# Bias rows of the first image's attention loaded and turned in separate steps, the opening reordered, and one later use in layer 1

## The chip, the cores and the metric

The kernel runs on one core of one Trainium2 chip. The metric is the device time of one execution in microseconds (us); lower is better. It ran three times: 3124.01 us in the median, 3123.47 at the lowest and 3126.42 at the highest. One further execution was recorded by the hardware profiler, and every duration of a single instruction comes from that one.

The core has engines that run side by side, each working through its own instructions in the order of the program: TensorE (PE, with its weight loads as PEld), VectorE (DVE), ScalarE (ACT), GpSimd (POOL) and SyncE (SP), which here issues nearly all the DMAs. They meet only at semaphores.

## What is computed

The input is 8 images of 384 channels with 32 x 32 pixels, that is 1024 tokens of 384 numbers each. Two layers follow one another. Everything is float32.

```
# layer 0, per image
x = x + attn0(group_norm(x))          # 8 heads of 48
#   attn = softmax(q k^T / sqrt(48) + bias[head, query, key]) ; out = attn v ; out @ proj_w + proj_b
#   bias = MLP(relative position of query and key)   -- the same for all images

# layer 1, on tokens t
t = t + attn1(layer_norm(t))          # 6 heads of 64
#   q = (q - mean) / std, k = (k - mean) / std over the 64 numbers of a head (ddof 1)
#   attn = softmax(q k^T / sqrt(64)) ; out = attn v ; out @ proj_w.T + proj_b
t = t + ffn(layer_norm(t))            # sign weights, absmax-quantised activations, GELU
#   the quantisation covers images 0 to 4; for images 5 to 7 the ffn gives zero
```

The bias depends only on the difference of two positions. So there are just 63 x 63 = 3969 values for each head: a small MLP over a table of positions makes them, and every score finds its bias by its offset in the table.

## The kernel before

**Units.** The attention of one image is cut into units `(pair, h, m2)`: a pair of heads, a half of the queries, and a quarter of the keys (256). Layer 0 has 4 x 2 x 4 = 32 units an image, layer 1 has 24. `scores` of a unit makes two PSUM tiles of 128 x 1024 on PE (L513); VectorE adds the bias to each (L524) and ScalarE takes the exponential (L528). `weigh` of a unit runs two units later (`LAG = 2`) and multiplies the exponentials by the values into an accumulator (L544). When a half of the queries is complete, ScalarE and VectorE bring the accumulator into `oT` (L552, L555); when a pair is complete, `divide` sends its sums through memory, GpSimd inverts them (L573), and the result is loaded again, spread over the partitions, and multiplied into `oT`. All PSUM tiles, those of projections and accumulators too, share one pool of four buffers (`mm2`).

**Order.** The order of every engine's work is the order of the statements. A hand-written clock spreads the small work between the large: `later.after(n, work)` does `work` at the n-th following call of `later.step()`. In image 0 of layer 0, `project_qk` calls it six times (after each projection of a pair's queries or keys), `project_v` four times, and then every unit once; so unit i ends with step 11 + i. At equal steps, work is done in the order in which it was registered.

**The opening.** The first image is loaded and its group norm measured (`stages[0]` to `stages[2]`). `hidden` makes the MLP's hidden layer (L350, L355), `stages[3]` sends the norm's scale and shift through memory, `table_part` makes each half of the bias table (L366, L371) and stores it in memory (L375), and `stages[4]` applies the norm on VectorE (L440). Then the weights for values and output are loaded, and projections follow (L459 queries and keys, L487 values).

**The bias.** `grow` holds the bias in the form in which the scores read it: for each of 8 heads, 60 rows of 32. It is filled in 32 parts `(head, c)` of 15 rows. For each part, `grow_part` issues four DMAs (L387), each of which fetches 32 shifted copies of a stretch of the table into a tile `wide` (117 KB each), and then one copy reads `wide` backwards into `grow`, on ScalarE for even `c` (L393) and on VectorE for odd `c` (L395). `wide` comes from a pool of nine tiles (`etile`), which also gives the hidden layer's tiles and the exponentials. A pair of heads needs 8 parts: pair 0 from unit 0 on, pair 1 from unit 8, pair 2 from unit 16, pair 3 from unit 24.

```python
for i in range(22):
    later.after(i + 1, lambda i=i: grow_parts(2 if i < 10 else 1))
```

**The next image.** After unit 1 of each image the next one is loaded (L252), and the stages of its group norm follow 5, 6, 7, 10 and 13 steps on (three times L410, then L424 and on, then L440 on GpSimd).

**Layer 1.** `attention_inputs` (L1562, the changed call is L1584) prepares an image's queries, keys and values for images 0, 6 and 7; for the others the feed-forward of the image before does it. `head(pair, a, b)` sums the squares of a pair's queries and keys on PE (L1157), sends them through memory, and takes the inverse root on GpSimd (L1178, 5.42 us). Then `apply` loads the queries' part as `rq` (L1192) `a` steps later, and the queries are multiplied by it on VectorE (L1199) `b` steps after that. Pair 2 is the last; its queries are used from unit 16 on. Tiles named by `wtile` come from a pool of 16.

Of the kernel before, what the change touches and what calls it, by code (L numbers as in the profile page):

```python
# [19 lines left out]
F32 = mybir.dt.float32  # L20
F32R = mybir.dt.float32r
AF = mybir.ActivationFunctionType
# [5 lines left out]
P = 128  # L28
QP = P // 2
B, C, IH, IW = 8, 384, 32, 32  # L30
# [10 lines left out]
NF0 = NP0 - 1  # L41
# [3 lines left out]
RW = 2 * IW - 1  # L45
# [7 lines left out]
NP1 = H1 // 2  # L53
# [43 lines left out]
class _Shared:  # L97
# [13 lines left out]
    def mm2(self, name):  # L111
        return self.ps.tile([P, NH, HALF], F32, tag="p", name=name)
# [71 lines left out]
def _layer0(tc, ins, x1, sums, shared, beside):  # L184
# [4 lines left out]
    nc = tc.nc  # L189
# [4 lines left out]
    with ExitStack() as ctx:  # L194
        const = ctx.enter_context(tc.tile_pool(name="a_const", bufs=1))
# [7 lines left out]
        def etile(name, shape=(P, N)):  # L203
            return ep.tile(list(shape), F32, tag="e", name=name)
# [4 lines left out]
        later = _Later()  # L209
# [8 lines left out]
        def backwards(last, *dims):  # L218

            dims = [(1, n) if isinstance(n, int) else n for n in dims]  # L220
            return bass.AP(last.tensor, last.offset, [last.ap[0]] + [[-s, n] for s, n in dims])
# [13 lines left out]
        for g in range(P // QT):  # L235
            at = g * QN
            n = min(QN, NREL - at)
# [80 lines left out]
        def load_weights_v_out():  # L318
            nc.sync.dma_start(wv, qkv_w[:, 2 * C : 3 * C].rearrange("(k p) c -> p k c", p=P))
            nc.sync.dma_start(bv, qkv_b[2 * C : 3 * C].partition_broadcast(P))  # L320
            pw = ins["L0_conv_proj_w"]
            for j in range(2):
                last = (2 * NF0 + j) * D0
                for row, n, at, step in (
                    (j * S0 + SP, D0, j * D0, 2 * D0),
                    (j * S0, FR, last, FR),
                ):
                    nc.sync.dma_start(
                        wp[row : row + n],
                        bass.AP(  # L330
                            pw.tensor, pw.offset + at * C, [[C, n], [step * C, NF0], [1, C]]
                        ),
                    )
                nc.sync.dma_start(wl[j * S0 + SP : (j + 1) * S0], pw[last : last + D0])
            with nc.allow_non_contiguous_dma(reason="a bias, once"):
                nc.sync.dma_start(bp, ins["L0_conv_proj_b"].rearrange("(k p) -> p k", p=P))

        oT = kept.tile([P, NP0, N], F32, tag="oT", name="oT")

        WR = GW // 4  # L340

        def hidden(r):

            hids = {}
            for k in range(2):
                for a in range(2):
                    ph = mm2(f"ph{r}{k}{a}")
                    for i in range(2):
                        g = 2 * a + i
                        nc.tensor.matmul(  # L350
                            ph[0:HC, i], w1[g * QT : g * QT + 2, ts(k, HC)],
                            rel[g * QT : g * QT + 2, ts(r, HALF)], start=True, stop=True,
                        )
                    hid = etile(f"hid{r}{k}{a}", (HC, 2, HALF))
                    nc.scalar.activation(  # L355
                        hid.rearrange("p i q -> p (i q)"), ph[0:HC].rearrange("p i q -> p (i q)"),
                        AF.Gelu, bias=b1[:, k : k + 1],
                    )
                    hids[k, a] = hid
            return hids  # L360

        def table_part(r, hids):
            pb = mm2(f"pb{r}")
            for k in range(2):
                for g in range(P // QT):
                    nc.tensor.matmul(  # L366
                        pb[ts(g, QT), 0], w2[:, k, :], hids[k, g // 2][:, g % 2],
                        start=(k == 0), stop=(k == 1),
                    )
            part = etile(f"part{r}", (P, HALF))  # L370
            nc.vector.tensor_scalar_add(backwards(part[:, HALF - 1 : HALF], HALF), pb[:, 0], b2)  # L371
            for g in range(P // QT):
                at = g * QN + r * HALF
                n = min(HALF, NREL - at)
                nc.sync.dma_start(  # L375
                    table[:, NREL - at - n : NREL - at],
                    part[g * QT : g * QT + H0, HALF - n : HALF],
                )

        def grow_part(h, c):  # L380

            run = (WR - 1) * RW + IW
            wide = etile(f"wide{h}_{c}", (P, WR, RW))
            for dy in range(QROWS):
                src = table[h : h + 1, :]
                at = src.offset + NREL - 1 - (WR * (c + 1) + QROWS - 2 - dy) * RW - 2 * (IW - 1)
                nc.sync.dma_start(  # L387
                    wide[ts(dy, IW)].rearrange("p w c -> p (w c)")[:, :run],
                    bass.AP(src.tensor, at, [[1, IW], [1, run]]),
                )  # L390
            turned = backwards(wide[:, WR - 1, IW - 1 : IW], (RW, WR), IW)
            if c % 2 == 0:
                nc.scalar.copy(grow[:, h, ts(c, WR), :], turned)  # L393
            else:
                nc.vector.tensor_copy(grow[:, h, ts(c, WR), :], turned)  # L395
# [240 lines left out]
        hids = [hidden(r) for r in range(2)]  # L636
        stages[3]()
        load_bias_qk()
        for r in range(2):
            table_part(r, hids[r])  # L640
        stages[4](nc.vector)
        load_weights_v_out()
        parts = [(h, c) for h in range(H0) for c in range(4)]

        def grow_parts(n):
            for _ in range(n):
                grow_part(*parts.pop(0))

        for i in range(22):
            later.after(i + 1, lambda i=i: grow_parts(2 if i < 10 else 1))  # L650
        qk = project_qk(0, first)
        project_v(0, first)
        with_last = beside(etile)
        for b in range(B):
            held = []
            for i, u in enumerate(units):
                done = held.pop(0) if len(held) == LAG else None
                held.append(
                    (u, scores(b, qk, u, lambda: weigh(b, *done) if done else None))
                )  # L660
                if i == 1 and b + 1 < B:
                    xn = load(b + 1)
                    for at, stage in zip((5, 6, 7, 10, 13), group_norm(b + 1, xn)):
                        later.after(at, stage)
                if i == 3 and b > 0:
                    project_out(b - 1, residuals(b - 1, etile), range(NF0))
                if b == B - 1:
                    for at, work in with_last:
                        if at == i:
                            work()  # L670
                later.step()
            if b + 1 < B:
                qk = project_qk(b + 1, xn)
            for done in held:
                finish = weigh(b, *done)
                if finish is not None:
                    finish()
            if b + 1 < B:
                project_v(b + 1, xn)
# [8 lines left out]
    def finish():  # L688
        project_out(B - 1, rest, range(NF0, NP0))
        keep.close()  # L690
# [319 lines left out]
def _layer1(tc, ins, x1, out, shared, start, before=None, check=None):  # L1010
# [3 lines left out]
    nc = tc.nc  # L1014
    with ExitStack() as ctx:
# [4 lines left out]
        const = pool("b_const", 1)  # L1020
# [5 lines left out]
        later = _Later()  # L1026
# [37 lines left out]
        wide = room = w1 = w2 = None  # L1064
# [10 lines left out]
        tiny = const.tile([P, 2], F32, tag="tiny", name="tiny")  # L1075
# [486 lines left out]
        def attention_inputs(b, xt, rest=()):  # L1562

            d, qk, sq = head_rows(b), {}, {}
            kc = kc_tile(b)
            tk = token_sums(f"a{b}", xt, [square(f"a{b}", xt, k) for k in range(KC)])

            def head(pair, *steps):
                head_sums(b, pair, sq, d)
                normalise_qk(b, pair, qk, d, kc, steps)  # L1570

            for pair in range(NP1):
                for s in range(2):
                    project_qk(b, pair, s, xt, qk, sq)
                    if (pair, s) == (0, 1):
                        token_stats(f"a{b}", tk)
                    if s == 0 and pair > 0:
                        head(pair - 1, *((3, 3) if pair == 1 else (5, 4)))
            for work in rest:
                work()  # L1580
                later.step()
            for m2 in range(MT // 2):
                project_v(b, xt, m2, tk)
            head(NP1 - 1, 3, 2)  # L1584
            return qk, kc

        def kc_tile(b):
# [19 lines left out]
        for b in range(B):  # L1607
# [4 lines left out]
            oT = None  # L1612
# [4 lines left out]
            for i, u in enumerate(units):  # L1617
# [7 lines left out]
                if i == 3:  # L1625
# [3 lines left out]
                    oT = wide.tile([P, KC, N], F32, tag="o", name=f"oT{b}")  # L1629
# [146 lines left out]
```

## Time and profile before

| what | value |
|---|---|
| median of the runs | 3124.01 us |
| the profiled execution | 3124.0 us |
| its span, first to last instruction | 3122.2 us |
| mean granted TensorE clock | 0.993 of full |
| VectorE add of the bias, L524 | 1218 ns |
| ScalarE exponential, L528 | 1057 ns |
| turning copy, ScalarE L393 / VectorE L395 | 593 / 653 ns (medians) |
| GpSimd inverse of the sums, L573 | 2899 ns |
| PE at work in 0 to 40 us | 30.03 us |
| PE at work in 80 to 100 us | 14.89 us |
| PE at work in 120 to 140 us | 7.34 us |

A busy time of an engine is the sum over its instructions. Since matmuls are pipelined, a busy PE need not be a fast PE: the row PEclk of the page, and the clock in the windows, say what share of the full clock TensorE had. An entry such as `DVE grow L395 <- DMA wide<-table: 54.1, 13, 10.8` in the list of waits reads: VectorE stood idle before its instruction of line 395, which writes `grow`, for 54.1 us in total, 13 times, 10.8 us at the longest, and each time a DMA from `table` into `wide` came last. In the timelines the columns are the start, the time taken, the engine, the line, the operation, what it writes and reads, how many were merged into the line, and the idle time before it with what ended it.

### The profile page before, as it was taken

The numbers are of one execution on the slowest core, as the hardware profiler recorded it, in microseconds if no ns is written. First come the engines' busy times: TensorE is split into PE (matmuls) and PEld (weight loads), VectorE is DVE, ScalarE is ACT, GpSimd is POOL, SyncE is SP. The second block draws the span as 40 slices with busy tenths as digits, with TensorE's granted clock in tenths as the row PEclk, the third lists the DMA queues.
The fourth block names the chain that finished last, engine by engine and source line by source line (L and its number), as shares of the span: only waits on it lengthen the run. The fifth ranks groups of instructions, "written<-read, shape, count | busy, mean of one in ns | idle before, by whom it ended". The sixth has DMA issues, their size and how long they took to land.

```text
span 3122.2 us, 45962 instructions
## 1 busy us (share of the span) xinstructions
PE 3049.8 (98%) x19066; PEld 1579.0 (51%) x19066; DVE 1736.5 (56%) x1735; ACT 1400.7 (45%) x1762; POOL 472.9 (15%) x314
## 2 busy tenths in 40 slices
PE   8799999999999999999899999999999999999998
PEld 3254645455554645434445645545645545544343
DVE  2564727364654737364554754754754854854545
ACT  2452616253443616243463553553643543653534
POOL 0110201111110202022201201201201201211110
PEclk9899999999999999999999999999999999999999
DMA  7402020111202020222300200101101101102011
GB/s 176 113 19 80 23 77 23 48 57 20 81 20 79 23 83 16 50 72 81 92 22 16 62 22 16 62 22 26 52 22 29 49 22 29 49 16 70 16 50 43
DMA packets 102771, 150.51 MB, mean 48 GB/s; under 512 B 62260, under 2 KB 65828, under 8 KB 101784
## 3 DMA queue, kind: packets, MB, share of 16 engines
q1 hardware_dynamic: 99688, 147.41, 16.8%
q8 instruction: 153, 2.51, 0.3%
q14 instruction: 66, 0.54, 0.1%
q10 hardware_dynamic: 2864, 0.05, 0.1%
HBM read 111.05 MB, written 27.32 MB: 44 GB/s over the span
## 4 chain that ended last, share of the span: by engine, by line
PE 84%; DVE 4%; DMA 3%; ACT 2%; POOL 1%; issue 1%; SPq 1%; DVEq 0%; ACTq 0%; POOLq 0%
PE s L513 14%; PE o L544 14%; PE s L1272 10%; PE o L1321 10%; PE pq L459 7%; PE y2p L1523 5%; PE pp L608 4%; PE y1p L1469 4%; PE pq L1128 4%; PE pp L1383 4%; PE pv L487 4%; PE pv L1209 3%; POOL hc L1178 1%; PE sum L1344 1%; DMA rb<-rd 1%
## 5 line engine op out<-in xcount | busy, mean ns | idle before, releaser
L528 ACT ACTIVATE e<-e 128x1024 f32<-128x1024 f32 x512 | 535.0, 1057 | 460.0 <-DVE e L524 444.2
L524 DVE TENSOR_TENSOR e<-s,grow 128x1024 f32<-128x1024 f32 x512 | 601.0, 1218 | 192.0 <-PE s L513 190.0
L513 PE MATMUL s<-qk 48*64 48x512 f32 x4096 | 615.4, 594 | 20.9 <-DVE e L524 17.2
L544 PE MATMUL o<-e,v 64*64 64x512 f32 x4096 | 609.8, 592 | 0.0
L1283 ACT ACTIVATE e<-s,kc 128x512 f32<-128x512 f32 x768 | 463.9, 691 | 203.4 <-PE s L1272 189.5
L1321 PE MATMUL o<-e,v 64*64 64x512 f32 x3072 | 393.5, 593 | 8.8 <-DVE oT L1331 8.8
L1272 PE MATMUL s<-qk,qk 64*64 64x512 f32 x3072 | 394.2, 592 | 2.2 <-DVE v L1219 1.9
L513 PEld LDWEIGHTS s<-qk 48*64 48x64 f32 x4096 | 235.1, 133 | 254.4 <-DVE e L524 86.3
L544 PEld LDWEIGHTS o<-e,v 64*64 64x64 f32 x4096 | 255.1, 133 | 185.9 <-issue 82.4
L1298 DVE TENSOR_TENSOR t<-t,e 128x1024 f32<-128x1024 f32 x192 | 231.0, 1222 | 77.4 <-ACT e L1283 77.4
L1128 PE MATMUL pq<-bx,wqkv 128*128 128x512 f32 x576 | 254.1, 596 | 0.7 <-ACT tra L1102 0.7
L459 PE MATMUL pq<-xn,w 128*128 128x512 f32 x576 | 251.0, 597 | 1.8 <-DVE xn L440 1.8
L573 POOL TENSOR_TENSOR inv<-sums,over 128x16 f32<-128x16 f32 x32 | 92.8, 2899 | 1029.5 <-DMA sums<-sd 872.1
L1272 PEld LDWEIGHTS s<-qk,qk 64*64 64x64 f32 x3072 | 144.1, 132 | 199.4 <-issue 123.2
L1321 PEld LDWEIGHTS o<-e,v 64*64 64x64 f32 x3072 | 140.1, 133 | 199.8 <-issue 161.0
L459 PEld LDWEIGHTS pq<-xn,w 128*128 128x128 f32 x576 | 109.4, 191 | 143.4 <-issue 143.4
L1128 PEld LDWEIGHTS pq<-bx,wqkv 128*128 128x128 f32 x576 | 107.8, 190 | 143.5 <-issue 141.4
L1295 DVE TENSOR_TENSOR t<-e,e 128x1024 f32<-128x1024 f32 x96 | 114.1, 1224 | 74.5 <-ACT e L1283 74.4
L1456 DVE TENSOR_REDUCE parts<-y 128x1 f32<-128x1024 f32 x75 | 90.1, 1217 | 99.1 <-ACT y L1453 98.6
L1144 ACT ACTIVATE qsq<-pq 128x1024 f32<-128x1024 f32 x48 | 49.2, 1024 | 195.1 <-DVE qk L1138 97.2
L1178 POOL TENSOR_TENSOR hc<-hc,rsqrt 128x32 f32<-128x32 f32 x24 | 135.6, 5649 | 2.0
L1209 PE MATMUL pv<-wqkv,bx 128*128 128x384 f32 x384 | 131.1, 497 | 0.0
(147 smaller groups left out, 2937.9 us busy)
## 6 DMA issues: line engine op xcount, KB each, us to landing
rb<-rd SPq DMA_DIRECT2D x112, 256.0 KB
wide<-table SPq DMA_DIRECT2D x128, 114.2 KB
xn<-in_x_dram SPq DMA_DIRECT2D x24, 512.0 KB
res<-in_x_dram SPq DMA_DIRECT2D x24, 512.0 KB
x<-res SPq DMA_DIRECT2D x24, 512.0 KB
bx<-x SPq DMA_DIRECT2D x8, 1536.0 KB
rq<-hi SPq DMA_DIRECT2D x48, 256.0 KB
out_dram<-bx SPq DMA_DIRECT2D x24, 512.0 KB
```

Source lines behind the costliest of these rows:

```text
L459: nc.tensor.matmul(pq[:, h], wqk[:, k, s, 2 * pair : 2 * pair + 2, :].rearrange("p h d -> p (h d)"), xn[:, k, ts(h, HALF)], start=(k == 0) ...
L513: nc.tensor.matmul(s[j][ts(c, QP), i], qk[pair][rows, 1, ts(4 * m2 + 2 * i + c, QP)], qk[pair][rows, 0, ts(h, HALF)], start=True, stop=True,)
L524: nc.vector.tensor_add(e.rearrange("p (i q) -> p i q", i=2), s[j], bass.AP(near.tensor, near.offset, [near.ap[0], [-QROWS * IW, 2], [1, HA ...
L528: nc.scalar.activation(e, e, AF.Exp)
L544: nc.tensor.matmul(po[ts(j, S0), r], v[keys, 2 * m2 + i, 2 * pair + j, :], es[j][keys, ts(i, HALF)], start=(m2 == 0 and i == 0), stop=(m2 ...
L1128: nc.tensor.matmul(pq[:, h], wqkv[:, k, s * C + pair * P : s * C + (pair + 1) * P], xt[:, k, ts(h, HALF)], start=(k == 0), stop=(k == KC - 1),
L1178: nc.gpsimd.tensor_tensor(c, c, rsqrt.to_broadcast(list(c.shape)), ALU.pow)
L1209: nc.tensor.matmul(pv[:, i, 0:C], xt[:, k].rearrange("c (p m) -> c m p", m=MT)[:, 2 * m2 + i], wqkv[:, k, 2 * C : 3 * C], start=(k == 0), ...
L1272: nc.tensor.matmul(s[j][ts(c, QP), i], qk[pair, 1][rows, ts(4 * m2 + 2 * i + c, QP)], qk[pair, 0][rows, ts(h, HALF)], start=True, stop=True,)
L1283: nc.scalar.activation(e[:, ts(i, HALF)], s[j][:, i], AF.Exp, scale=kc[:, pair, j, m : m + 1])
L1298: nc.vector.tensor_add(total[j], total[j], e)
L1321: nc.tensor.matmul(po[ts(j, D1), r], v[keys, 2 * m2 + i, at : at + D1], es[j][keys, ts(i, HALF)], start=(m2 == 0 and i == 0), stop=(m2 == ...
```

## The change

There are three edits.

1. **The opening.** The norm is applied (`stages[4]`) and the weights are loaded before the bias table's first half; the second half is made one step later, after the first projection. A tile `tiny` and one exponential of it on ScalarE are added.
2. **The bias.** `grow_part` is split: `grow_load` issues the four DMAs, `grow_turn` makes the copy. Twenty parts are loaded at steps 2 to 9 (three each at the first four steps, then two) and turned one step later (first four groups) or two steps later (the rest). The other twelve are loaded one a step at steps 8 to 19 and turned one a step at steps 11 to 22; these don't use the pool of nine but three slices of `oT`, in turn. With this, image 1 is loaded after unit 8 of image 0, not after unit 1.
3. **Layer 1.** For the last pair in `attention_inputs`, the steps of `head` are (4, 4) and not (3, 2).

```diff
+        tiny = const.tile([P, 2], F32, tag="tiny", name="tiny")
+        nc.gpsimd.memset(tiny, 0.0)
...
-        def grow_part(h, c):
+        def grow_load(h, c, staged):
 
             run = (WR - 1) * RW + IW
-            wide = etile(f"wide{h}_{c}", (P, WR, RW))
+            wide = oT[:, staged, 0 : WR * RW] if staged else etile(f"wide{h}_{c}", (P, WR * RW))
             for dy in range(QROWS):
...
+            return wide
+
+        def grow_turn(h, c, wide):
+
+            last = (WR - 1) * RW + IW - 1
+            turned = backwards(wide[:, last : last + 1], (RW, WR), IW)
             if c % 2 == 0:
                 nc.scalar.copy(grow[:, h, ts(c, WR), :], turned)
...
         load_bias_qk()
-        for r in range(2):
-            table_part(r, hids[r])
         stages[4](nc.vector)
         load_weights_v_out()
+        table_part(0, hids[0])
+        later.after(1, lambda: table_part(1, hids[1]))
+        nc.scalar.activation(tiny[:, 1:2], tiny[:, 0:1], AF.Exp)
         parts = [(h, c) for h in range(H0) for c in range(4)]
-
-        def grow_parts(n):
+        waiting = []
+
+        def grow_loads(n, staged=None):
             for _ in range(n):
-                grow_part(*parts.pop(0))
-
-        for i in range(22):
-            later.after(i + 1, lambda i=i: grow_parts(2 if i < 10 else 1))
+                part = parts.pop(0)
+                waiting.append((*part, grow_load(*part, staged)))
+
+        def grow_turns(n):
+            for _ in range(n):
+                grow_turn(*waiting.pop(0))
+
+        for i, n in enumerate((3, 3, 3, 3, 2, 2, 2, 2)):
+            later.after(i + 3 + (i > 3), lambda n=n: grow_turns(n))
+            later.after(i + 2, lambda n=n: grow_loads(n))
+        for i in range(len(parts) - 20):
+            later.after(i + 11, lambda: grow_turns(1))
+            later.after(i + 8, lambda i=i: grow_loads(1, 1 + i % NF0))
...
-                if i == 1 and b + 1 < B:
+                if i == (8 if b == 0 else 1) and b + 1 < B:
                     xn = load(b + 1)
...
-            head(NP1 - 1, 3, 2)
+            head(NP1 - 1, 4, 4)
```

More of the change, by code (lines that the diff above doesn't have):

```diff
@@ L387, in grow_part @@
                 nc.sync.dma_start(
-                    wide[ts(dy, IW)].rearrange("p w c -> p (w c)")[:, :run],
-                    bass.AP(src.tensor, at, [[1, IW], [1, run]]),
-                )
-            turned = backwards(wide[:, WR - 1, IW - 1 : IW], (RW, WR), IW)
+                    wide[ts(dy, IW), 0:run], bass.AP(src.tensor, at, [[1, IW], [1, run]])
+                )
+            return wide
+        def grow_turn(h, c, wide):
+            last = (WR - 1) * RW + IW - 1
+            turned = backwards(wide[:, last : last + 1], (RW, WR), IW)
             if c % 2 == 0:
```

## The prediction

> **What bounds the kernel now.** I read the page first, then the waits and the windows of the opening 160 us, the timelines of PE, VectorE, ScalarE and SyncE there, and last the one place in layer 1 that the third edit touches. The page:
>
> ```profile
> PE 3049.8 (98%) x19066; PEld 1579.0 (51%) x19066; DVE 1736.5 (56%) x1735; ACT 1400.7 (45%) x1762; POOL 472.9 (15%) x314
> ...
> PE   8799999999999999999899999999999999999998
> ...
> PEclk9899999999999999999999999999999999999999
> ```
>
> TensorE is the bound: a microsecond counts only where PE stands still or runs at half clock. The PE row shows that in slices 1 and 2 (78 us each) and slice 20, so only the first image of layer 0 and the start of layer 1 have anything to give. Who waits for whom in 0 to 160 us (us in total, times, longest):
>
> ```profile
> ACT grow L393 <- DMA wide<-table: 55.7, 11, 18.5
> DVE grow L395 <- DMA wide<-table: 54.1, 13, 10.8
> ...
> PEld s L513 <- DVE e L524: 27.3, 14, 12.4
> ...
> PE s L513 <- DVE e L524: 17.2, 6, 11.5
> ```
>
> Each part of the bias is loaded and turned in one step, so the turning copy waits on its engine for the whole transfer, with evictions, bias adds and exponentials behind it. VectorE where units 0 and 9 of the scores stand behind a copy:
>
> ```profile
> 79.90 0.65 DVE L395 COPY grow<-wide 128x480 f32<-128x480 f32 x1 [2.42 <-DMA wide<-table]
> 80.47 1.01 DVE L492 TENSOR_TENSOR v<-pv,bv 128x384 f32<-128x384 f32 x2
> 84.06 0.65 DVE L395 COPY grow<-wide 128x480 f32<-128x480 f32 x1 [2.58 <-DMA wide<-table]
> 84.63 4.61 DVE L524 TENSOR_TENSOR e<-s,grow 128x1024 f32<-128x1024 f32 x4
> ...
> 136.80 0.65 DVE L395 COPY grow<-wide 128x480 f32<-128x480 f32 x1 [10.80 <-DMA wide<-table]
> ```
>
> The copy at 136.80 came late because SyncE stood for seven microseconds (126.03 to 132.6) inside `divide`, with the part's loads behind it. The windows (us, busy time and count of PE, PEld, DVE, ACT, POOL, granted clock, DMA share, GB/s):
>
> ```profile
> 40.00:60.00 20.00, 20.00 (x48) 8.87 (x47) 4.99 (x6) 4.40 (x6) 0.00 (x0) 1.00 1.00 220
> ```
> ```profile
> 84.00:88.00 4.00, 2.10 (x9) 0.87 (x13) 3.94 (x4) 2.05 (x3) 0.00 (x0) 0.50 0.98 324
> ...
> 134.00:138.60 4.60, 0.00 (x0) 0.00 (x0) 1.80 (x3) 0.00 (x0) 0.00 (x0) 0.50 0.63 187
> ...
> 150.00:215.40 65.40, 65.40 (x607) 37.91 (x607) 48.48 (x44) 42.29 (x44) 12.96 (x5) 1.00 0.07 18
> ```
>
> The DMA engines are full while the bias comes in, and from 150 us PE runs without a gap: 3.44 us a unit (1.72 scores, 1.72 weighing). The values' projection ends at 76.4, so without stalls units 0 to 31 would end at 76.4 + 2 x 1.72 + 30 x 3.44 = 183.0; they end at 215.4, where PE begins image 1's `pq`. So 32.4 us are lost there, and some in front. In layer 1, PE and then VectorE:
>
> ```profile
> 1539.70 2.84 PE L1272 MATMUL s<-qk,qk 64*64 64x512 f32 x16
> 1551.34 3.49 PE L1321 MATMUL o<-e,v 64*64 64x512 f32 x16 [8.79 <-DVE oT L1331]
> ```
> ```profile
> 1546.99 1.23 DVE L1199 TENSOR_TENSOR qk<-qk,rq 128x1024 f32<-128x1024 f32 x1 [7.79 <-DMA rq<-hi]
> 1548.32 2.36 DVE L1295 TENSOR_TENSOR t<-e,e 128x1024 f32<-128x1024 f32 x2
> 1550.60 0.68 DVE L1331 TENSOR_TENSOR oT<-o,oT 128x512 f32<-128x512 f32 x1
> ```
>
> The multiply by the last pair's deviations waits 7.79 us for its load; behind it stands the eviction of the weighing's accumulator, for which PE waits.
>
> **What the Trainium skill says.** "TensorE: Matmul & The Clock Gate", Architectural detail (engine queue depths): ScalarE and VectorE are strict FIFOs. The trace agrees: the ready adds of 84.63 start only after the copy. The same page, Part 1, says that after an idle window of about 3.4 us the array runs at half clock until it has been busy about as long. It agrees: PEclk is 0.50 at 84 to 92 and 134 to 142, and an L513 matmul takes 1.06 us there, 0.59 elsewhere. "DMA: Bandwidth & Descriptors", Anatomy of one DMA, says that a DMA's semaphore wait is served on the issuing sequencer; SyncE's standstill in `divide` is that.
>
> **The opening.** Applying the norm moves ahead of the table, and the table's second half behind the first projection. `pb` starts at 20.01 as before; its 32 matmuls took 6.25 us, so the first half ends at about 23.1. The scale `gsc` was issued at 17.16; image 1's was usable 1.66 us after its 0.39 us issue, so VectorE applies 19.2 to 21.6 (3 x 0.804), hidden under PE's work. `pq` starts at 23.1, not 28.05, and PE's 1.79 us gap is gone, as is the half clock of 28.7 to 32.1 (`pq`'s 72 records took 32.4 us here, 31.1 in image 1). The second half adds its 3.1 us after the first `pq`. Values' projection done: 23.1 + 31.0 + 3.1 + 15.7 = 72.9, that is 3.5 earlier. The `Exp` of `tiny` moves a 1.28 us table load from 82.62 to about 22; ScalarE waits at both, so nothing.
>
> **When parts land.** SyncE now issues the 11 weight DMAs (4.4 us) before the table stores, then waits for the second half: PE 31.4, VectorE's 0.75, four stores to 34.1, and I estimate 1.9 us to land, from the 1.66 above and the 2.45 that a late part took. First part: 36.0 + four issues 1.7 + 2.3 = 40.0 (before: 40.56). Then the engines' rate rules: before, part 19 was turned at 84.06, so (84.06 - 40.56 - 3 x 1.2 for the `qk` copies) / 19 = 2.1 us a part. Part 17 lands at about 78.6, 19 at 82.7, 20 at 84.8, 21 at 86.9, 23 at 91. Image 1's 1.5 MB, issued at 82.5 before amid the parts, now come at unit 8.
>
> **Units 0 to 4.** Turns come one to three steps behind loads, but the transfers lag the steps, so some copies still wait. (Unit i is step 11 + i.) VectorE: part 17 to 79.3, add of unit 0 to 81.7, part 19 to 83.4, unit 1 to 85.7, part 21 to 87.6, unit 2 to 89.9. ScalarE: part 20 at 84.8 precedes unit 1's exponentials. PE has four PSUM buffers, so scores of unit 3 wait for the first add of unit 2 (88.7). By then PE has been mostly idle since 74.6: half clock, and 88.7 + 3.4 for the scores + 3.4 for the weighing + 1.7 puts the end of unit 4's scores at 97.2; fully warm it would be 93.9. From there 27 units of 3.44 and one weighing: 97.2 + 92.9 + 1.7 = 191.8, or 188.5 warm. I take 191.4: 24.0 us off 215.4, the 3.5 included.
>
> **What does not come back.** Staged parts (12 of 32) use `oT` slices 1 to 3; each load waits for the copy three parts earlier, issued in the same step, which costs SyncE a short stand and leaves 10.3 us for about 4.4 us of issue and landing. The last load is issued at unit 8, the first `divide` at unit 9, so the standstill of 126 has no part behind it. The last part queues behind image 1's load: 7 us of transfer at 220 GB/s against three units; if that cover failed, VectorE would wait 1 to 3 us once. Slice 1 is first written with results at unit 13, after its last turn at unit 9. The norm of image 1 now measures at units 12 to 14 (VectorE 2.4 + 1.3 us a unit, as in later images, with buffers between) and applies at unit 20 on GpSimd, 11 units before use. Its stores and loads on SyncE meet `divide` of pair 1 at unit 17; nobody waits for either.
>
> **Layer 1.** With (4, 4) the load of `rq` is issued at unit 3 and the multiply at unit 7 instead of 2 and 4. SyncE reached that load at 1540.66, held by the chain before it and not by the step, so it lands at 1547 again; unit 7's adds come no earlier, so the wait is gone. Next late is the order that stays: exponentials of unit 5 done 1540.5, add to 1541.7, eviction 1542.4, weighing from 1542.5 instead of 1551.34: 8.8 us, plus 1.6 for the half clock that made it 3.3 us apart instead of 1.72: 10.4. Bounds: 8.8 (clock stays down) to 11.5 (PE without any gap from 1541.4). The multiply's 1.22 us in unit 7 stand before unit 8, which has no VectorE adds. Images 6 and 7 turn from unit 4 to unit 7 too, where no PE wait stood: 0.
>
> **Sum.** The profiled execution took 3124.0 us (span 3122.2, 1.8 around it), the median is 3124.01. 3124.0 - 24.0 - 10.4 = 3089.6.
>
> **Rivals.**
> 1. Transfers rule harder: the parts land 6 us later than I put them, because the table is complete later (34 instead of 28.5) and its landing is only estimated. Every unit shifts one for one: 3095.6. Against: SyncE did not start loading before 34.07 anyway.
> 2. The layer 1 edit gives nothing, because the accumulator waits for something else: 3100. Against: the three VectorE lines above follow each other without a gap.
> 3. Everything is hidden: units at PE's pace from 72.9, end at 179.5, 11.5 in layer 1: 3124.0 - 35.9 - 11.5 = 3076.6. Against: it needs part 21 at unit 1 (78 us), impossible at 2.1 us a part.
> 4. Slower: the `oT` slices are ordered as one tile, so that each staged DMA waits for the last one's landing. Place: SyncE, steps 8 to 19. Price: 4 x 2.45 = 9.8 us a part, 12 parts from 73 to 191, then 20 units: end 260, 44 us later, less layer 1's 10.4: 3158. It decides from (215.4 + 10.4 - 68.8 - 73) / 12 = 7.0 us a part. Against: the four loads of one `wide` tile go out 0.5 us apart, and `xn`'s first slice is measured while the others land.
>
> **Numbers.** Forecast 0.63 (own range 3084 to 3095: landing by 2 us either way, clock, 8.8 to 11.5), rival 1 0.17, rival 2 0.09, rival 3 0.06, rival 4 0.04, and 0.01 that gain and loss cancel. Range 3082 to 3100. A change of 0.2% (6 us) is about what this measurement can tell. Faster 0.95, same 0.01, slower 0.04.
>
> **What would show it.** Right: `pq` starting near 23; part 0 turned at 40 to 42; no VectorE wait on `wide` after 95; image 1's `pq` starting near 191; no wait before L1199 near unit 7 in layer 1. Wrong: PE gaps after unit 5, SyncE waiting long before staged loads, part 0 landing after 44, or the weighing in layer 1 still waiting for L1331.

## The result, and the profile after

The changed kernel took 3088.35 us in the median of four runs (3085.19 to 3088.45), the kernel before, beside it, 3124.82 us. The ratio is 0.9881, with a 95% interval of 0.9864 to 0.9898: 36.5 us less. The profiled execution of the changed kernel is its fastest, 3085.19 us, with a span of 3083.4; before it was 3124.0 and 3122.2. Line numbers shift: L513 is now L521, L524 is L532, L393 and L395 are L401 and L403, L387 is L391, and in layer 1 L1199 is L1220 and L1331 is L1352.

The page of the changed kernel:

```profile
PE 3039.7 (99%) x19066; PEld 1582.6 (51%) x19066; DVE 1736.9 (56%) x1735; ACT 1400.0 (45%) x1763; POOL 472.1 (15%) x315
...
PE   8999999999999999999999999999999999999998
...
PEclk9999999999999999999999999999999999999999
```

The dips of slices 2 and 20 are gone; only the very start and the very end are left. VectorE and ScalarE are busy for as long as before. The waits of its first 160 us (us in total, times, longest):

```profile
ACT grow L401 <- DMA wide<-table: 24.5, 9, 4.5
...
DVE grow L403 <- DMA wide<-table: 19.1, 8, 4.6
...
PEld s L521 <- DVE e L532: 14.4, 24, 2.8
...
PE s L521 <- DVE e L532: 2.6, 3, 1.9
```

The turning copies still wait for their parts, 45 us in all where it was 110 (1.2 us of it for parts in `oT`), but none for longer than 4.6 us, and PE waited 2.6 us for an add where it waited 17.2. VectorE at units 0 to 3, and PE where it waits for these adds:

```profile
77.33 0.65 DVE L403 COPY grow<-wide 128x480 f32<-128x480 f32 x1 [2.64 <-DMA wide<-table]
77.91 2.35 DVE L532 TENSOR_TENSOR e<-s,grow 128x1024 f32<-128x1024 f32 x2
...
84.88 0.65 DVE L403 COPY grow<-oT 128x480 f32<-128x480 f32 x1 [1.19 <-DMA oT<-table]
85.45 2.35 DVE L532 TENSOR_TENSOR e<-s,grow 128x1024 f32<-128x1024 f32 x2
88.70 2.36 DVE L532 TENSOR_TENSOR e<-s,grow 128x1024 f32<-128x1024 f32 x2 [0.91 <-PE s L521]
```
```profile
79.17 4.44 PE L521 MATMUL s<-qk 48*64 48x512 f32 x16 [1.95 <-DVE e L532]
...
86.72 1.51 PE L521 MATMUL s<-qk 48*64 48x512 f32 x11 [0.54 <-DVE e L532]
```

The copy of 84.88 is the last one on VectorE that waits for its part. The add of unit 2 stands behind it, and PE's scores of unit 3 wait for that add until 86.72. After that the adds wait for PE; the other way round there is one wait of 0.15 us, at 128.49. SyncE around the first `divide`:

```profile
107.18 1.32 SPq L252 DMA_DIRECT2D xn<-in_x_dram  x3
109.91 1.90 SPq L391 DMA_DIRECT2D oT<-table  x4
112.40 0.52 SPq L578 DMA_DIRECT2D sd<-oT  x2
115.71 0.35 SPq L580 DMA_DIRECT2D sums<-sd  x1
120.28 0.34 SPq L582 DMA_DIRECT2D rd<-inv  x1
```

It still stands for eight microseconds between 112.4 and 120.3, but the last loads of the bias went out at 109.91, ahead of it, and PE waits for nothing that is behind it. In layer 1, PE and then VectorE:

```profile
1511.84 2.92 PE L1293 MATMUL s<-qk,qk 64*64 64x512 f32 x16
1514.68 1.95 PE L1342 MATMUL o<-e,v 64*64 64x512 f32 x16
```
```profile
1513.94 0.68 DVE L1352 TENSOR_TENSOR oT<-o,oT 128x512 f32<-128x512 f32 x1
...
1523.49 1.22 DVE L1220 TENSOR_TENSOR qk<-qk,rq 128x1024 f32<-128x1024 f32 x1
```

The weighing follows the scores without a gap, the accumulator is evicted at 1513.94, and the multiply comes ten microseconds later and waits for nothing.

So the two places divide the gain like this. Image 1's first projection on PE starts at 187.16 instead of 215.40: 28.2 us. The scores before the layer 1 wait start at 1511.84 instead of 1539.70, 27.9 us, and those after it at 1516.45 instead of 1554.65, 38.2 us: 10.3 us between the two. The end keeps it: the last projection starts at 3068.76 instead of 3107.69, 38.9 us.

### The profile page after: what moved, and what is told of

It is laid out like the page before. It is cut to its first block, busy times and chain, and to the rows that moved or that the text cites. A ratio compares the mean times of both kernels' runs of the same rounds, so it can differ in the third digit from the quotient of the medians.

```text
span 3083.4 us, 45983 instructions
## 1 busy us (share of the span) xinstructions
PE 3039.7 (99%) x19066; PEld 1582.6 (51%) x19066; DVE 1736.9 (56%) x1735; ACT 1400.0 (45%) x1763; POOL 472.1 (15%) x315
## 4 chain that ended last, share of the span: by engine, by line
PE 87%; DVE 4%; DMA 3%; ACT 2%; issue 1%; SPq 1%; POOL 1%; DVEq 0%; ACTq 0%; POOLq 0%
PE s L521 14%; PE o L552 14%; PE s L1293 11%; PE o L1342 10%; PE pq L467 8%; PE y2p L1544 5%; PE pp L616 4%; PE y1p L1490 4%; PE pp L1404 4%; PE pv L495 4%; PE pq L1149 4%; PE pv L1230 3%; SPq L391 1%; PE sum L1365 1%; POOL hc L1199 1%
## 5 line engine op out<-in xcount | busy, mean ns | idle before, releaser
L532 DVE TENSOR_TENSOR e<-s,grow 128x1024 f32<-128x1024 f32 x512 | 601.4, 1218 | 190.4 <-PE s L521 189.8
L521 PE MATMUL s<-qk 48*64 48x512 f32 x4096 | 612.4, 592 | 2.7 <-DVE e L532 2.6
L521 PEld LDWEIGHTS s<-qk 48*64 48x64 f32 x4096 | 237.0, 132 | 228.5 <-issue 76.3
L1199 POOL TENSOR_TENSOR hc<-hc,rsqrt 128x32 f32<-128x32 f32 x24 | 135.4, 5642 | 2.0
```

What stands on the lines that cost most here:

```text
L521: nc.tensor.matmul(s[j][ts(c, QP), i], qk[pair][rows, 1, ts(4 * m2 + 2 * i + c, QP)], qk[pair][rows, 0, ts(h, HALF)], start=True, stop=True,)
L532: nc.vector.tensor_add(e.rearrange("p (i q) -> p i q", i=2), s[j], bass.AP(near.tensor, near.offset, [near.ap[0], [-QROWS * IW, 2], [1, HA ...
L1199: nc.gpsimd.tensor_tensor(c, c, rsqrt.to_broadcast(list(c.shape)), ALU.pow)
```

## The experiments

Each kernel ran beside the kernel before on the same chip, in three groups; medians of the kernel before were 3130.22, 3127.15 and 3124.52 us. The changed kernel ran again in the second group. "Start" is where PE begins image 1's projection in the profiled execution, which tells the first image's share apart from the rest.

| run | what it is | median us | ratio to before (95%) | start us |
|---|---|---|---|---|
| (before) | the kernel before | 3124.82 | | 215.40 |
| (after) | the changed kernel | 3088.35 | 0.9881 (0.9864 to 0.9898) | 187.16 |
| e1 | changed, layer 1 steps (3, 2) | 3099.64 | 0.9902 (0.9887 to 0.9917) | 188.18 |
| e2 | changed, image 1 loaded after unit 1 | 3089.18 | 0.9874 (0.9859 to 0.9889) | 189.08 |
| e3 | changed, old opening | 3089.50 | 0.9873 (0.9858 to 0.9888) | 188.94 |
| e4 | changed, first 20 turned at once, rest later | 3101.14 | 0.9910 (0.9896 to 0.9923) | 199.51 |
| e7 | changed, again | 3089.62 | 0.9879 (0.9864 to 0.9894) | 190.25 |
| e5 | changed, last 12 turned at once | 3101.54 | 0.9922 (0.9909 to 0.9936) | 202.46 |
| e6 | paced by landings | 3079.89 | 0.9851 (0.9837 to 0.9864) | 182.60 |
| e8 | changed, first 20 turned at once, rest by threes | 3095.61 | 0.9899 (0.9883 to 0.9914) | 195.73 |
| e9 | before, image 1 loaded after unit 8 | 3116.75 | 0.9975 (0.9964 to 0.9985) | 209.08 |
| e10 | before, layer 1 steps (4, 4) | 3114.95 | 0.9970 (0.9959 to 0.9981) | 213.48 |
| e11 | paced, GELU table early | 3077.79 | 0.9850 (0.9837 to 0.9864) | 182.22 |

### The changed kernel again (e7)

No edit.

> The changed kernel itself, as the yardstick for the others on this chip: within 0.1% of the ratio that it had, 0.988 of the kernel before.

The ratio is 0.9879. But its profiled execution starts image 1 at 190.25, 3.1 us later than the first profile. VectorE and PE in this run:

```profile
84.84 0.66 DVE L403 COPY grow<-wide 128x480 f32<-128x480 f32 x1 [1.94 <-DMA wide<-table]
...
88.04 0.65 DVE L403 COPY grow<-oT 128x480 f32<-128x480 f32 x1 [0.28 <-DMA oT<-table]
88.61 2.35 DVE L532 TENSOR_TENSOR e<-s,grow 128x1024 f32<-128x1024 f32 x2
```
```profile
89.90 1.92 PE L521 MATMUL s<-qk 48*64 48x512 f32 x16
```

The parts came later. The first one is turned at 39.82 instead of 38.87, because the first twelve `pq` took 1.1 us longer (7.61 instead of 6.55) and the table waited with them. Part 19 is turned at 84.84 instead of 80.77 and part 21 at 88.04 instead of 84.88. So the add of unit 2 is later, and the scores of unit 3, which wait for it, start at 89.90 instead of 86.72. These 3.2 us are the whole difference. Why the transfers were slower in this execution is not known.

The clock differs too. The windows of units 0 to 4 (columns as in the prediction), first of the first profile, then of this one:

```profile
73.60:90.00 16.40, 13.85 (x99) 4.44 (x102) 11.07 (x13) 8.33 (x11) 0.00 (x0) 0.90 0.89 224
```
```profile
73.60:90.00 16.40, 13.64 (x72) 3.81 (x74) 9.37 (x12) 6.43 (x9) 0.00 (x0) 0.79 0.97 237
```

PE is equally busy in both, but with a clock of 0.79 it gets through 72 matmuls instead of 99. The half clock came for 6.8 us here and for 3.4 us there. It is not what makes the difference: in both runs it lay in front of the scores of unit 3, in time that PE would otherwise have spent waiting for the add of unit 2 (its first half ended at 89.8 here). So one kernel can end three microseconds apart by when its parts land; this is about the distance between the first run of the changed kernel (3085.19) and its other three (3088.34 to 3088.45), of which no profile was taken.

### Layer 1 alone, taken back and put in (e1, e10)

```diff
-            head(NP1 - 1, 4, 4)
+            head(NP1 - 1, 3, 2)
```

> The changed kernel with the last pair's steps in layer 1 put back to (3, 2). Theory (the multiply's wait holds the accumulator's eviction, 10.3 us): slower than the changed kernel by 9 to 11.5 us, about 3098.5, with the multiply in unit 4 waiting some 7.8 us for its load again and PE idle about 8.8 us before the weighing. Rival (the wait was a by-product of when layer 0 ended, and after the earlier end the load lands in time): within 2 us of the changed kernel.

> The kernel before with the layer 1 edit alone. Theory (it is independent of the rest): faster than the kernel before by 9 to 11.5 us, as putting it back in the changed kernel cost some 10. Rival (part of it comes only together with the rest): faster by less than 7 us.

Taken back it costs 10.0 us (3099.64 to e7's 3089.62; they ran in different groups, and by the ratios it is 7.2; e2 and e3 below, which ran in its own group and equal the changed kernel, are 10.5 and 10.1 us faster than it). Put into the kernel before it gives 9.6 us (3124.52 to 3114.95). Both agree with the 10.3 of the traces. In e1 the old wait is back; PE, then VectorE:

```profile
1524.30 3.69 PE L1342 MATMUL o<-e,v 64*64 64x512 f32 x16 [8.55 <-DVE oT L1352]
```
```profile
1519.95 1.23 DVE L1220 TENSOR_TENSOR qk<-qk,rq 128x1024 f32<-128x1024 f32 x1 [7.54 <-DMA rq<-hi]
1521.28 2.36 DVE L1316 TENSOR_TENSOR t<-e,e 128x1024 f32<-128x1024 f32 x2
1523.56 0.68 DVE L1352 TENSOR_TENSOR oT<-o,oT 128x512 f32<-128x512 f32 x1
```

The multiply waits 7.54 us for `rq`, the add and the eviction follow, and PE starts the weighing when the eviction is over. The rivals (a by-product, or a gain that needs the other edits) fall.

### The last twelve parts turned in the step of their load (e5)

```diff
         for i in range(len(parts) - 20):
-            later.after(i + 11, lambda: grow_turns(1))
-            later.after(i + 8, lambda i=i: grow_loads(1, 1 + i % NF0))
+            later.after(i + 11, lambda i=i: (grow_loads(1, 1 + i % NF0), grow_turns(1)))
```

> The changed kernel with the last twelve parts loaded and turned in the same step, at steps 11 to 22 as before, still into the slices of oT; the first twenty as in the changed kernel. Theory (the loads of units 9 to 11 stand on SyncE behind divide of unit 9, which serves its waits in order): one copy at unit 9 or 10 waits 9 to 13 us, PE stands and falls to half clock, 10 to 16 us slower than the changed kernel. Rival (three slices let SyncE run ahead of the steps, so the place of the load in the order costs nothing): within 3 us of the changed kernel.

11.9 us slower than e7. SyncE, VectorE and PE:

```profile
114.89 0.52 SPq L578 DMA_DIRECT2D sd<-oT  x2
116.43 0.34 SPq L580 DMA_DIRECT2D sums<-sd  x1
121.09 0.34 SPq L582 DMA_DIRECT2D rd<-inv  x1
121.53 5.92 SPq L391 DMA_DIRECT2D oT<-table  x12
```
```profile
125.86 0.65 DVE L403 COPY grow<-oT 128x480 f32<-128x480 f32 x1 [11.01 <-DMA oT<-table]
```
```profile
127.70 2.83 PE L521 MATMUL s<-qk 48*64 48x512 f32 x11 [10.63 <-DVE e L532]
```

The three parts of units 9 to 11 (12 DMAs) leave SyncE only after `rd`, which waits for GpSimd. The copy waits 11.01 us, PE 10.63, and PE then takes 2.83 us for eleven matmuls, at half clock. The rival was right for units 0 to 8, where SyncE does run ahead of the steps (its loads up to part 28 were out by 103.6), and wrong at the one place where the queue stands.

### The first twenty turned in the step of their load (e4, e8)

```diff
-        for i, n in enumerate((3, 3, 3, 3, 2, 2, 2, 2)):
-            later.after(i + 3 + (i > 3), lambda n=n: grow_turns(n))
-            later.after(i + 2, lambda n=n: grow_loads(n))
+        for i in range(10):
+            later.after(i + 1, lambda: (grow_loads(2), grow_turns(2)))
```

In e4 the other twelve keep their three steps, but are loaded at steps 11 to 22. In e8 they are loaded by threes at steps 11, 13, 15 and 17 and turned two steps later.

> The changed kernel with the first twenty parts loaded two a step at steps 1 to 10 and turned in the same step, as before; the other twelve are staged in oT and turned three steps after their loads (loads at steps 11 to 22, turns at 14 to 25). Theory (the copies of the first twenty wait for transfers that run at full rate either way): part 19 is turned near 81, unit 0's add follows at 81.5, and later parts no longer hold anything up, so within 3 us of the changed kernel, 3086 to 3091. Rival (the early split is what pays): slower by 6 us or more, above 3094.

> The first twenty parts loaded and turned in one step, two a step, as before; the last twelve staged in oT by threes at steps 11, 13, 15 and 17 and turned two steps later, so that no load comes behind divide. Theory (the run with late loads lost most of its time at unit 12, to divide, and only some 3 us to the copies made at once): slower than the changed kernel by 2 to 5 us. Rival (turning at once is the main loss): slower by 8 us or more, as the run with late loads was.

e4 missed its range: 11.5 us slower than e7. But the run had two edits in one: its last loads had moved behind `divide`, a copy at unit 12 waited 5.2 us for them at 131, PE stood as long, and then ran at half clock from 134.4 to 140.7, which is another 3.2 us. That leaves some 3 us. e8 has no load behind `divide` and is 6.0 us slower, between the two expectations. VectorE before unit 0 in e8:

```profile
82.61 0.65 DVE L403 COPY grow<-wide 128x480 f32<-128x480 f32 x1 [2.80 <-DMA wide<-table]
83.18 4.61 DVE L532 TENSOR_TENSOR e<-s,grow 128x1024 f32<-128x1024 f32 x4
```

With the copies of all twenty parts ahead of it, unit 0's add starts at 83.18 instead of 77.91 (80.6 in e7), and the half clock lasts 13.7 us instead of 3.4 to 6.8. But e8 has a second edit too, and it costs: with the last twelve loaded by threes and a lead of two steps, VectorE waits for another part, and PE for VectorE:

```profile
117.58 0.65 DVE L403 COPY grow<-oT 128x480 f32<-128x480 f32 x1 [2.61 <-DMA oT<-table]
```
```profile
119.42 1.51 PE L521 MATMUL s<-qk 48*64 48x512 f32 x11 [1.93 <-DVE e L532]
```

With a smaller wait at 103.20 (0.36 us) these are 2.3 of the 6.0 us. So the early split is worth 3 to 4 us by both runs, a third of what the late one is. This is an estimate from the traces; no run has the early copies at once and the last twelve as in the changed kernel.

### The opening, and the place of image 1's load (e3, e2, e9)

```diff
+        for r in range(2):
+            table_part(r, hids[r])
         stages[4](nc.vector)
         load_weights_v_out()
-        table_part(0, hids[0])
-        later.after(1, lambda: table_part(1, hids[1]))
```

> The changed kernel with the old order of the opening (both halves of the table, then the norm, then the weights); the early exponential stays. Theory (units 0 to 4 are ruled by when the parts land, so the 3 to 3.5 us that PE is earlier are mostly lost again; what counts is the landing of part 0, 1.7 us earlier in the changed kernel): slower by 1 to 2.5 us, 3089.5 to 3091, projections starting near 28 and part 0 turned near 40.5. Rival (PE's order rules): slower by 3.5 to 5 us.

> The changed kernel with image 1 loaded after unit 1 again, not after unit 8. Theory (transfers rule units 0 to 4: 1.5 MB are 7 us of the DMA engines, in front of the parts 23 and later): those parts land about 7 us later, their copies at units 3 and 4 wait 3 to 6 us, 3 to 6 us slower than the changed kernel, about 3093. Rival (three steps between load and copy cover it): within 1.5 us of the changed kernel.

> The kernel before with one part of the change alone: image 1 loaded after unit 8. Theory (a transfer of 7 us costs wherever copies have no lead on their loads): the wait of the copy of part 21 (4.4 us, and the half clock around it) goes, but the transfer now stands ahead of the last parts and the standstill in divide stays, so within 5 us of the kernel before either way. Rival (the place of this load is itself a main part of the gain): faster by 8 us or more.

In e2 the changed kernel loads image 1 after unit 1 again. Neither e3 nor e2 can be told from the changed kernel (3089.50 and 3089.18 beside 3089.62); with intervals of 0.0015 to each side of the ratios, some 5 us could hide there, so the traces have to decide. In e3 the values' projection ends at 75.6 instead of 73.6 and part 19 is turned at 82.67 instead of 80.77, yet image 1 starts at 188.94, between the two profiles of the changed kernel. The loss of 1 to 2.5 us that was expected is neither shown nor excluded. In e2 the image's 1.5 MB do come between the parts (issued at 85.98), but no copy waits after 85.6: the three steps of lead cover it. There the rival was right.

In the kernel before, moving the load to unit 8 gives 7.8 us (4.7 to 11.2 by the interval of the ratio), more than I allowed, and so nearer to the rival. Of its eight runs the profiled one was the slowest (3122.86), so only the first image is read from it: it starts image 1 at 209.08, 6.3 us earlier than before. (Part of that is lost again in layer 1, where PE waits 10.8 us for the accumulator in this execution, and 8.8 before.) The standstill remains in it:

```profile
132.12 0.65 DVE L395 COPY grow<-wide 128x480 f32<-128x480 f32 x1 [10.80 <-DMA wide<-table]
```

So the place of this load is worth some 8 us where copies have no lead on their loads and nothing where they have.

### A version paced by the landings (e6), and its opening (e11)

The changed kernel still lost about 7 us in units 0 to 4 (9 in e7). In e6 the number of turns in each step follows the landings seen in the profile. This needs more room for parts under way: three slices of the image buffer that is free between image 0's last projection and image 1's load, which moves to unit 11.

```diff
+        turns = {3: 2, 4: 2, 5: 2, 6: 3, 7: 2, 8: 2, 9: 1, 10: 2,
+                 11: 1, 12: 1, 13: 2, 14: 1, 15: 2, 16: 1, 17: 2, 18: 1, 19: 2, 20: 1, 21: 2}
+        loads = {2: 4, 3: 3, 4: 3, 5: 3, 6: 3, 7: 2, 8: 2}
+        slots = {8: (1,), 9: (2,), 10: (3,), 11: (4, 5, 6), 14: (1,), 15: (2, 3), 16: (4,),
+                 17: (5, 6)}
...
-                if i == (8 if b == 0 else 1) and b + 1 < B:
+                if i == (11 if b == 0 else 1) and b + 1 < B:
```

> A version meant to take the rest: the same loads, but every copy is put where its part has landed by the times of the changed kernel's profile (2 a step in the projections, 1 or 2 a unit up to unit 10), twenty parts through the pool of nine and twelve through oT's three slices and the three slices of the image buffer that is free until image 1 is loaded, which moves to unit 11. Theory (only copies ahead of their transfers hold PE in units 0 to 4): units run at PE's pace from the values' projection on, image 1's projection starts near 180 to 182, 6 to 10 us less than the changed kernel. Rival (the DMA engines' rate or the four PSUM buffers hold PE there in any order): within 3 us of the changed kernel.

9.7 us faster than e7, and faster than both kernels: 0.9851 of the kernel before. PE from the end of the values' projection to image 1:

```profile
73.83:182.60 108.77, 108.67 (x993) 57.83 (x993) 89.14 (x89) 72.15 (x78) 20.66 (x13) 1.00 0.37 97
```

PE is busy for 108.67 of 108.77 us at full clock, where 106.6 would be the least. The rivals (rate, PSUM buffers) fall: with the DMA engines as full as in the changed kernel and the same four buffers, PE runs through when, from unit 0 on, no copy is put ahead of its part.

In e11 a GELU of `tiny` loads the table at the start, and five loads move from ScalarE's queue to SyncE's:

```diff
+        nc.scalar.activation(tiny[:, 1:2], tiny[:, 0:1], AF.Gelu)
...
-            nc.scalar.dma_start(b2[g * QT : g * QT + H0], ins["L0_conv_mlp_b2"].unsqueeze(1))
+            nc.sync.dma_start(b2[g * QT : g * QT + H0], ins["L0_conv_mlp_b2"].unsqueeze(1))
```

> The paced version, with the opening's chain shortened: the GELU table is loaded on ScalarE at the start (a GELU of the tile tiny), and the five small loads of the second MLP weight and bias are issued by SyncE, not by ScalarE ahead of the first GELU. Theory (the first GELU at 13.8 us waits for ScalarE's own DMA issues, to 12.4, and then for the table load of 1.28): GELUs start near 10.5 to 11, the table, the first part and the first projection come 1.5 to 3 us earlier, and so does the end: 3077 to 3078.5 where the paced version takes 3080. Rival (the norm's scale, usable at 18.8, or TensorE's half clock of the opening holds the projection): within 1 us of the paced version.

```profile
0.73 1.28 ACT L228 ACT_TABLE_LOAD   x1 [0.73 <-PEq L1805]
...
7.84 3.89 SPq L291 DMA_DIRECT2D b<-in_L_conv_mlp_b_dram  x4
...
11.76 1.11 ACT L359 ACTIVATE hid<-ph,b 96x1024 f32<-96x1024 f32 x1 [9.54 <-DMA b<-in_L_conv_mlp_b_dram]
...
11.83 0.40 SPq L424 DMA_DIRECT2D there<-gst  x1
...
21.17 2.26 DVE L450 TENSOR_SCALAR xn<-xn,gsc 128x1024 f32<-128x1024 f32 x3 [4.88 <-DMA gsc<-back]
```

The first GELU starts at 11.76 instead of 13.80, but the moved loads now hold SyncE before the norm's statistics (11.83, in e6 8.43), so the norm is applied 2.3 us later. The projections still end 2.9 us earlier, and then copies wait for their parts again: image 1 starts at 182.22 instead of 182.60. The median is 2.1 us lower, but the ratios to the kernel before, 0.9850 and 0.9851, don't tell the two apart. Inconclusive.

## Why the prediction was right, point by point

- **Layer 1**: 10.4 predicted, 10.3 in the trace, and the cause as given: the eviction queued behind a waiting multiply.
- **The opening**: the projection starts at 23.8 (23.1 predicted) and the values' projection ends at 73.6 (72.9). Two errors hide in this. I expected full clock from the first `pq` on; PE in the changed kernel shows otherwise:

```profile
20.23 3.64 PE L370 MATMUL pb<-hid,w 96*32 96x512 f32 x16
23.80 6.55 PE L467 MATMUL pq<-xn,w 128*128 128x512 f32 x12
30.28 1.92 PE L370 MATMUL pb<-hid,w 96*32 96x512 f32 x16
32.14 26.02 PE L467 MATMUL pq<-xn,w 128*128 128x512 f32 x60
```

  Twelve `pq` records take 6.55 us at first and 5.2 later, and the table's second half takes 1.9 us, not the 3.1 that I took from a stretch at half clock. That the errors cancel is luck. That these 3.5 us are hardly a gain of their own, since the landings rule, fits e3, which could not be told from the changed kernel.
- **Landings**: the first part is turned at 38.87, not 40.0, and part 21 at 84.88, not 86.9 (in e7 at 39.82 and 88.04). The table's second half was ready a little later than predicted, at 32.2 on PE and not 31.4, and its last store ended at 34.4, not 34.1. But its landing, an estimate of 1.9 us, was too long: the loads follow at 34.7. With the 3.6 us for the `qk` copies taken off, a part took 2.02 us in one profile and 2.12 in the other, so the rate of 2.1 held. The working had two slips: 21 parts at 2.1 us after 40.0 give 87.7, not 86.9, and the weight DMAs are nine, not 11 (their 4.4 us are right).
- **Units 0 to 4**: 24.0 us predicted for the first image, 28.2 in one profile and 25.2 in the other. The wait was the right one: the scores of unit 3 stand behind the add of unit 2, and that behind part 21. They went on at 86.72 and at 89.90, where 88.7 was predicted. What was wrong is the half clock after it: I put 3.4 us for the next two blocks at half speed, but in both profiles the half clock had ended (at 84.1 and 89.6), and in e7 unit 3's sixteen records took 1.9 us. So this term was some 3 us too much, and the gain in it too small. In the first profile the earlier landing adds 2.0 us to that; in e7 a later one takes 1.2 back, and that the forecast fits e7 best is luck again.
- **What sets the clock**: the rates are as the prediction says, 1.06 us for an L513 matmul at half clock and 0.59 at full. But it also says that the trace agrees with a half clock that follows an idle window of about 3.4 us, and the trace does not show that. The clock fell at 83.3 before and at 80.7 in the changed kernel, and in the 10 us in front of it PE has a single gap: 1.95 us in the changed kernel (the line of 79.17 above), and in the kernel before this one:

```profile
81.63 2.03 PE L513 MATMUL s<-qk 48*64 48x512 f32 x14 [2.54 <-DVE v L492]
```

  The other dip of the kernel before began at 127.7, when its long gap was 0.6 us old. In e3 the clock fell at 81.9, after a gap of 0.99 us (79.2 to 80.2); in e8 a gap of 1.93 us in front of 119.42 left it at full. What decides is open here.
- **What was said not to come back** did not: no wait before a staged load that anyone feels, nothing behind `divide`, no wait of the last pair's multiply in images 6 and 7.
- **The rivals**: later landings (the first part came 1.1 us earlier than predicted, not 6 later), an empty layer 1 edit, and slices of `oT` ordered as one tile (four staged loads leave SyncE in 1.90 us) are all refuted by the trace. The third, all of it hidden, needed another placement of the copies; e6, with the same transfers, starts image 1 at 182.6, three microseconds from the 179.5 priced for it. "Impossible at 2.1 us a part" was true of the changed order only.
- **The sum**: 34.4 us less predicted, 36.5 measured.

What the prediction did not say is which part of the second edit carries the gain. The runs do in part: loads ahead of `divide` 11.9 us, the early split 3 to 4. These and layer 1's 10 make 25 to 26 of the 36.5. The remaining 11 or so go to no single part: the image's load costs nothing when moved back alone, and moving it alone in the old order gives 7.8. My reading, which no run shows, is that a lead on the loads and a transfer moved out of the way remove the same wait, so that each finds it gone once the other is made; which of the edits takes the rest was not separated.

## What to carry to other kernels

Place a consumer that shares an in-order engine with critical work by when its data land, from the trace, and not a fixed number of steps behind the load. Before a chain of store, load and compute on the queue that issues the DMAs, send off everything that will be needed during it. And price edits that cover the same wait together: alone, each can look worthless in one order and worth much in another.

## What the hardware did that was not expected

TensorE ran at half speed in the opening although the profile counts it as busy from 11.2 us on: `pb` took 3.64 us for sixteen records at 20 us and 1.92 at 30, while the clock column of the windows says 1.00 throughout. Busy does not mean without a pause here: up to 20 us its weight loads wait 5 us in all for ScalarE's GELUs (1.6 us at the longest). But from 20.2 on the matmuls follow one another, and full speed still came only some microseconds later, and not at the same time in each execution: the first twelve `pq` records took 6.55 us in one profile of the changed kernel and 7.61 in the other, and 5.42 in e11, beside 5.2 at full speed. If what they took more is put down to half speed, they ran so for 2.7, 4.8 and 0.4 us (an estimate), that is until about 26.5, 28.5 and 22.8. The matmuls ahead of `pq` use 2 or 96 rows. Whether the small matmuls, the pauses or something else is the reason was not tried.
